# Two-layer graph kernel: first features in halves, first slab as a corner and a rest, eight warming products

## The chip, the cores and the metric

The kernel runs on one core of a Trainium2 chip. The metric is the device time of one execution in microseconds (us); the number shown for a kernel is the median of its runs. A profile is one further execution, recorded by the hardware profiler; the stretch from its first to its last recorded work is the span, and all times in profile lines count from the start of the span.

The core has a matrix engine (PE, "TensorE", whose weight loads are listed apart as PEld), a vector engine (DVE, "VectorE"), a scalar engine (ACT, "ScalarE"), a general engine (POOL) and SP, which here only issues transfers. Transfers between the chip's memory and the core are carried by 16 DMA engines and are issued here from SP's and from ACT's instruction stream (their queues).

## What is computed

Two graph layers on features x of 8 x 2048 x 64 with a normalized adjacency `adj` of 2048 x 2048, each followed by a layer norm over the sum with its input:

```python
def reference(x, adj, L0_gnn_embedding, L0_gnn_weight, L0_gnn_bias, L1_gnn_weight, L1_gnn_bias):
    # layer 0: I, A, 2 A A - I applied to x, node-wise weights from an embedding
    ...
        x_g = jnp.einsum('knm,bmc->bnkc', A_stack, x)
        out = jnp.einsum('bnki,nkio->bno', x_g, w)
        return out + b
    ...
    x = _layernorm(x + _L0_gnn_ref(x, adj, ...), axis=-1)
    # layer 1: x, A x, 2 A A x - x, for two supports (both are adj), shared weights
    x = _layernorm(x + _L1_gnn_ref(x, adj, adj, L1_gnn_weight, L1_gnn_bias), axis=-1)
    return x
```

All entries of a row of `adj` that are not zero are equal, so the kernel multiplies by a matrix of ones and zeros and scales the rows afterwards.

## The kernel before

Features lie in 16 tiles of 128 nodes (partitions) by 512 values (8 batches by 64 channels). `in_x` holds them in this layout; `in_adj` holds the transposed adjacency as [half of the targets, source tile, 128 sources, 1024 targets]. The program has four passes over the adjacency, one after another on PE: the first hop (lines 544 to 613, `hop_x`), the second (seven products of quarters, line 623), the mixing of layer 0 (line 413), and layer 1's two hops (lines 880 and 1011 on).

The change lies wholly in the start of the first hop. `hop_x(g, kk, j)` handles source tile k = kk + 8 j against quarter g of each half of the targets, that is 2 x 512 targets in 8 blocks of 128. In time the sources come in the order 0, 8, 1, 9, 2, 10 and so on, first for g = 0, then for g = 1, together 32 steps. A step has three parts, which `run` (line 279) calls ahead of time by a lead: `features` (lead 4, transfers), `operands` (lead 2, casts) and `use` (lead 0, the products). Instructions of one engine stay in the order in which these parts call them (`ordered`, `keep_in_program_order`).

- **Features.** A float32 tile is split into two parts for the matrix engine: `high` (line 247) copies it on ACT into `hl[0]` in the rounded type fp32r; `low` (line 250) subtracts that on DVE into `hl[1]`. Tile 0 is loaded by `first_constants` (line 134) from ACT's queue, and tile 8 and the later ones from SP's.
- **Slab.** The adjacency rows of the source tile for the 2 x 512 targets are loaded into `raw` and turned into ones and zeros in `s` on DVE. For source tiles 0 and 8 in g = 0 (the branch `if g == 0 and kk == 0`) the two halves of 512 targets are separate transfers (`load_slab` in `features`, line 551) and separate DVE operations (line 562); all later steps load 2 x 512 in one and turn them in one operation (`places`, line 235).
- **Products.** `add_block` (line 262) issues 16 products a step: for each of the 8 blocks i of 128 targets, one with `hl[0]` and one with `hl[1]`, both over 512 columns. In a step they come block by block, high then low; in the first step of a pass (`first`) the eight high ones come before the eight low ones.
- **Warming products.** `first_constants` issues WARM products of a tile of zeros (`idle`) before the first real ones; nobody reads their result, but they occupy the accumulator bank that blocks 6 and 7 use in the first step.
- **Waits of transfers.** `load` (line 124) keeps the order of each queue. The raw slabs share a pool of 6 buffers (RAW), the operands `s` one of 4 and the feature parts `hl` one of 7, so that a later load or cast waits until an earlier buffer has been used.

On SP's queue the order at the start is: the two half slabs of tile 0, the features of tile 8, the two half slabs of tile 8, the features of tile 1, the whole slab of tile 1, the features of tile 9, and so on. On ACT's queue: the features of tile 0 and then the small array `rcol`. ACT then loads its table for the square root (line 139) and runs the casts.

On DVE the order is: half slab 0 of tile 0, low part of tile 0, half slab 1 of tile 0, low part of tile 8, half slabs 0 and 1 of tile 8, slab and low part of tile 1, then the four operations of `put_together` (line 536), which make sums of pairs of slabs for the second hop, and slab and low part of tile 9. On ACT: high parts of tiles 0, 8 and 1, then `seen` (line 601), a counted bf16 copy of each slab, between the later high parts.

Of the kernel before, what the change touches and what calls it, by code (L numbers as in the profile page):

```python
# [14 lines left out]
ALU = mybir.AluOpType  # L15
# [3 lines left out]
P = 128  # L19
B, N, C = 8, 2048, 64  # L20
# [5 lines left out]
FIRST = 8  # L26
HL = 7
RAW = 6
WARM = 10
SLOTS = 3  # L30
SPLIT = 4096.0
SWAPPED = (0, 2, 1, 3, 4, 6, 5, 7)
# [9 lines left out]
def pattern(  # L42
# [22 lines left out]
    nc = tc.nc  # L65
# [20 lines left out]
    def bank(name):  # L86

        return psum.tile([P, 2, 512], F32, tag="ps", name=name)
# [7 lines left out]
    z = [z0, [z1[:, t, :] for t in range(NT)], [z2[:, t, :] for t in range(NT)]]  # L96

    def bc(s, t):
        return z[s][t].rearrange("p (b c) -> p b c", c=C)
# [24 lines left out]
    def load(q, to, src):  # L124
        return tc.keep_in_program_order(q.dma_start(out=to, in_=src))
# [3 lines left out]
    def ordered(ins):  # L129
        if in_order:  # L130
            tc.keep_in_program_order(ins)


    def first_constants():
        load(nc.scalar, z[0][0], x[0].rearrange("n b c -> n (b c)"))
        load(nc.scalar, rcol, rcols)
        nc.vector.memset(eps, EPS)

        tc.keep_in_program_order(nc.scalar.activation(root, eps, AF.Sqrt))

        idle = spool.tile([P, 5 * P], BF16, tag="s", name="idle")
        nc.vector.memset(idle, 0.0)
        first = bank("first")
        for _ in range(WARM):
            nc.tensor.matmul(first[:, 0, :], lhsT=idle[:, :P], rhs=idle[:, P:], start=True, stop=True)
        nc.vector.memset(part, 1.0 / C)
        make_identity(nc, ident)
# [77 lines left out]
    def load_slab(src, shape):  # L225
        raw = rawp.tile(shape, F32, tag="raw", name="raw")
        load(nc.sync, raw, src)
        return raw
# [6 lines left out]
    def places(raw):  # L235
        s = spool.tile(list(raw.shape), F32R, tag="s", name="s")
        ordered(nc.vector.tensor_scalar(s, raw, 0.0, None, ALU.not_equal))
        return s
# [8 lines left out]
    def high(src, to):  # L247
        ordered(nc.scalar.copy(to[0], src))  # L248

    def low(src, to):  # L250

        ordered(nc.vector.tensor_tensor(to[1], src, to[0], ALU.subtract))  # L252

    def halves(src, to=None):

        if to is None:
            to = [hpool.tile([P, B * C], F32R, tag="hl", name="hl") for _ in range(2)]
        high(src, to)
        low(src, to)
        return to  # L260

    def add_block(accs, s, hl, first, last):

        order = [(i, h) for i in range(len(accs)) for h in range(2)]
        if first:
            order.sort(key=lambda ih: ih[1])
        for i, h in order:
            nc.tensor.matmul(  # L268
                accs[i], lhsT=s[:, i * P : (i + 1) * P], rhs=hl[h],
                start=(first and h == 0), stop=(last and h == 1),  # L270
            )
# [19 lines left out]
    def banks(n):  # L291
        pairs = [bank("acc") for _ in range(n // 2)]
        return [p[:, i] for p in pairs for i in range(2)]
# [107 lines left out]
    def centre_features(t):  # L401
        s = work.tile([P, B], F32, tag="ln_s", name="s")
        ordered(nc.vector.tensor_reduce(s, bc(0, t), AX.X, ALU.add))  # L403
        ordered(nc.gpsimd.tensor_tensor(s, s, part, ALU.mult))  # L404
        ordered(nc.gpsimd.tensor_tensor(bc(0, t), bc(0, t), wide(s), ALU.subtract))
# [110 lines left out]
    Q = N // 4  # L516
    BC = B * C // 2
    KK = NT // 2
    first_constants()


# [3 lines left out]
    quarters = scratch.tile([KK, P, 2, 2, Q], BF16, tag="quarters", name="quarters")  # L525
    corner = scratch.tile([KK, P, 2, Q], BF16, tag="corner", name="corner")
    couple, due, stores = [], [], []

    def put_together(g, kk, x0, x1):
        to = z2[:, 2 * (kk % 8) : 2 * (kk % 8) + 2, :].rearrange("p t n -> p (t n)").bitcast(BF16)  # L530
        to = to.rearrange("p (i n) -> p i n", i=4)
        for i, (a, b, op) in enumerate((
            (x0[:, 1], x1[:, 1], ALU.add), (to[:, S1], x0[:, 0], ALU.subtract),
            (x1[:, 0], to[:, S2], ALU.subtract), (x0[:, 0], x0[:, 1], ALU.subtract),
        )):
            ordered(nc.vector.tensor_tensor(to[:, i], a, b, op))

        stores.append(lambda: ordered(nc.scalar.dma_start(out=sums_of[kk, g], in_=to)))

        for _ in range(2):  # L540
            if len(stores) > (1 if g else 6):
                stores.pop(0)()

    def hop_x(g, kk, j):
        k = kk + KK * j

        def features(got):
            if g == 0 and kk == 0:
                if j == 1:
                    load(nc.sync, z[0][k], x[k].rearrange("n b c -> n (b c)"))  # L550
                got["raws"] = [load_slab(adj[h, k, :, :Q], [P, Q]) for h in range(2)]

        def operands(got):
            if g == 0 and kk == 0:

                s = got["s"] = spool.tile([P, 2, Q], F32R, tag="s", name="s")
                hl = got["hl"] = [hpool.tile([P, B * C], F32R, tag="hl", name="hl") for _ in range(2)]
                high(z[0][k], hl)
                if j == 1:
                    low(z[0][k], hl)  # L560
                for h in range(2):
                    ordered(nc.vector.tensor_scalar(s[:, h], got["raws"][h], 0.0, None, ALU.not_equal))
                    if h == 0 and j == 0:
                        low(z[0][k], hl)
            else:
                if g == 0:
                    load(nc.sync, z[0][k], x[k].rearrange("n b c -> n (b c)"))
                raw = load_slab(adj[:, k, :, g * Q : (g + 1) * Q].rearrange("h m n -> m h n"), [P, 2, Q])
                got["s"] = places(raw)
                got["hl"] = halves(z[0][k])  # L570
                if g == 1 and len(loads) > 3:
                    load(nc.sync, *loads.pop(0))
            while due:
                due.pop(0)()
            couple.append(got["s"])
            if j == 1:
                due.append(lambda both=couple[:]: put_together(g, kk, *both))
                couple.clear()
                if g == 1 and kk == KK - 1:
                    due.pop(0)()  # L580

        def out(i):
            t = 4 * g + i if i < 4 else 4 * g + i + 4
            a, r = accs[i], rcol[:, t : t + 1]
            if i % 2 if g == 0 or i > 3 else i > 1:
                ordered(nc.vector.tensor_scalar_mul(z[1][t], a, r))
            else:
                ordered(nc.scalar.activation(z[1][t], a, AF.Copy, scale=r))

        def use(got):  # L590
            s, hl = got["s"], got["hl"]
            if kk == 0 and j == 0:
                accs[:] = banks(8)
            last = kk == KK - 1 and j == 1
            add_block(accs, s.rearrange("p h n -> p (h n)"), hl, kk == 0 and j == 0, last)
            if last:
                for i in range(8 if g == 0 else 4):
                    out(i)
            seen = xcpool.tile([P, 2, Q], BF16, tag="ln_xc", name="seen")
            i = g * NT + k  # L600
            ordered(nc.scalar.activation(seen, s, AF.Copy, accum_out=nonzero[:, i : i + 1]))
            if j == 1:
                ordered(nc.scalar.dma_start(out=quarters[kk, :, :, g, :], in_=seen))
            else:
                ordered(nc.scalar.dma_start(out=corner[kk, :, g, :], in_=seen[:, 0]))
            if k in centred and g == 1:
                centre_features(k)
            if last and g == 1:
                stores.pop(0)()

                todo.extend(lambda i=i: out(i) for i in range(4, 8))

        return [(4, features), (2, operands), (0, use)]


# [142 lines left out]
    accs, centred = [], []  # L758
# [141 lines left out]
    s = ("load_sum", "operands")  # L900
    h, norm = None, None
# [3 lines left out]
    for t in range(NT):  # L905
        got, last = {}, t == NT - 1
# [62 lines left out]
        norm, h = norm_now, z[0][t]  # L969
# [435 lines left out]
def gnn_kernel(tc, x, xT, adj, diag, rcols, bias, pack, w0, out):  # L1405
    nc = tc.nc
    with tc.tile_pool(name="flag", bufs=1) as fpool:
        flag = fpool.tile([1, 1], I32, tag="flag", name="flag")
        odd = pattern(tc, x, xT, adj, diag, rcols, bias, pack, w0, out, flag)
        with tc.If(odd > 0):  # L1410
            general(tc, x, adj, bias, pack, w0, out)
# [45 lines left out]
```

## Time and profile before

| what | value |
|---|---|
| median of 3 runs | 751.47 us (751.16 to 751.69) |
| profiled execution | 751.04 us |
| its span | 749.2 us |
| PE busy | 740.5 us (99% of the span) |
| PEld, DVE, ACT, POOL busy | 613.4, 598.5, 456.6, 293.9 us |
| granted TensorE clock over the span | 0.997 |
| all transfers | 96.47 MB, mean 129 GB/s |
| line 268, products of the first hop (`acc`) | 512, 116.6 us |

How to read it: PE is busy almost all the time, so the order of time along PE is the whole program. Where a line in the profile carries a bracket, it gives the time for which the engine stood idle just before, and what released it. "x47" means that 47 instructions in a row are merged into one line. SPq and ACTq are the instruction streams that issue transfers.

The early transfers and DMA share, in windows of the profile:

```profile
0.00:5.18 5.18, 3.68 (x11) 1.24 (x11) 0.85 (x5) 2.10 (x3) 0.70 (x6) 1.00 0.61 198
5.18:8.00 2.82, 2.82 (x12) 2.13 (x13) 1.95 (x4) 0.62 (x1) 0.00 (x0) 1.00 0.96 300
8.00:12.00 4.00, 4.00 (x19) 3.34 (x18) 1.98 (x5) 2.36 (x5) 0.00 (x0) 1.00 1.01 384
```

The columns are the window, its length, the busy time (and count) of PE, PEld, DVE, ACT and POOL, the granted clock, the mean busy share of the DMA engines, and GB/s.

### The profile page before, as it was taken

What the parts mean: (1) busy time and instruction counts of PE and PEld (TensorE: products, weight loads), DVE (VectorE), ACT (ScalarE), POOL (GpSimd) and SP (SyncE); (2) the same over time, 40 slices, a digit from 0 to 9 for tenths busy, and PEclk for the clock granted to TensorE, in tenths of its full rate; (3) what the DMA queues carried; (4) which work ended last, traced back from release to release, by engine and by line L of the source; (5) the groups of instructions that cost most, each with busy time, mean ns of one, the idle gap of its engine ahead of it and who ended that gap; (6) DMA issues with size and microseconds to landing.
All of it is one profiled execution on the core that took longest, in us unless ns stands there. A gap on an engine that the chain in (4) does not pass through costs nothing.

```text
span 749.2 us, 13523 instructions
## 1 busy us (share of the span) xinstructions
PE 740.5 (99%) x4940; PEld 613.4 (82%) x4940; DVE 598.5 (80%) x952; ACT 456.6 (61%) x1123; POOL 293.9 (39%) x314
## 2 busy tenths in 40 slices
PE   9999999999999999999999999999999999999996
PEld 6888888888888888888888888888888888888885
DVE  6868887999978898888888888869588457778563
ACT  5545453878756678777777777778877662012111
POOL 0001111133233888888888888874000000021431
PEclk9999999999999999999999999999999999999998
DMA  8996997555420000000000000004454454665621
GB/s 301 365 381 214 380 397 243 177 159 166 157 86 15 17 15 16 20 15 26 11 20 15 16 15 1 2 29 131 135 159 151 129 170 139 180 183 171 198 98 46
DMA packets 73544, 96.47 MB, mean 129 GB/s; under 512 B 4864, under 2 KB 48384, under 8 KB 73344
## 3 DMA queue, kind: packets, MB, share of 16 engines
q1 hardware_dynamic: 62064, 76.66, 32.5%
q10 hardware_dynamic: 11408, 18.89, 6.8%
q8 instruction: 41, 0.67, 0.4%
q14 instruction: 31, 0.25, 0.1%
HBM read 76.65 MB, written 18.87 MB: 127 GB/s over the span
## 4 chain that ended last, share of the span: by engine, by line
PE 98%; DMA 0%; DVE 0%; ACT 0%; issue 0%; DVEq 0%; ACTq 0%
PE pm L424 35%; PE accT L705 27%; PE acc L268 16%; PE a L268 10%; PE accT L268 6%; PE pu L499 3%; PE pt L314 1%; PE accT L861 1%; DMA z<-in_x 0%; PE accT L499 0%; PE accT L155 0%; PE accT L314 0%; ACT hl L248 0%; DVE z L303 0%; DVE sq L1076 0%
## 5 line engine op out<-in xcount | busy, mean ns | idle before, releaser
L705 PE MATMUL accT<-s,hl 128*128 128x512 f32 x896 | 205.8, 391 | 0.0
L705 PEld LDWEIGHTS accT<-s,hl 128*128 128x128 f32 x896 | 167.5, 188 | 35.5 <-issue 0.5
L458 ACT ACTIVATE aside<-pm,pack_sb 128x128 f32<-128x128 f32 x512 | 141.9, 437 | 18.9 <-PE pm L424 16.3
L424 PE MATMUL pm<-wh,hl 64*128 64x512 f32 x768 | 151.7, 392 | 0.0
L424 PE MATMUL pm<-wm,parts 64*128 64x512 f32 x768 | 149.8, 387 | 0.0
L424 PE MATMUL pm<-wl,parts 64*128 64x512 f32 x768 | 149.7, 386 | 0.0
L692 ACT CAST s<-raw 128x1024 fp32r<-128x1024 bf16 x104 | 110.1, 1059 | 36.8 <-ACT hl L248 27.9
L268 PE MATMUL acc<-hl,s 128*128 128x512 f32 x512 | 116.6, 390 | 0.2 <-ACT hl L248 0.2
L474 DVE TENSOR_REDUCE sums<-aside 128x128 f32<-128x1024 f32 x96 | 112.6, 1214 | 1.4
L268 PEld LDWEIGHTS acc<-hl,s 128*128 128x128 f32 x512 | 95.8, 188 | 21.0 <-ACT hl L248 0.7
L445 DVE TENSOR_TENSOR aside<-pm,pack_sb 128x1024 f32<-128x1024 f32 x64 | 78.0, 1222 | 18.5 <-PE pm L424 18.1
L424 PEld LDWEIGHTS pm<-wm,parts 64*128 64x128 f32 x768 | 72.0, 184 | 15.3
L424 PEld LDWEIGHTS pm<-wh,hl 64*128 64x128 f32 x768 | 72.2, 185 | 14.7 <-issue 0.4
L424 PEld LDWEIGHTS pm<-wl,parts 64*128 64x128 f32 x768 | 72.2, 184 | 14.4
L248 ACT CAST hl<-z 128x256 fp32r<-128x256 f32 (+1 forms) x96 | 47.9, 517 | 58.6 <-PE acc L268 23.9
L268 PE MATMUL a<-hl,s 128*128 128x512 f32 (+1 forms) x352 | 73.4, 370 | 0.0
L404 POOL TENSOR_TENSOR s<-s,part 128x8 f32<-128x8 f32 x16 | 7.0, 439 | 166.0 <-DVE s L403 95.4
L252 DVE TENSOR_TENSOR hl<-z,hl 128x512 fp32r<-128x512 f32 (+1 forms) x96 | 58.1, 613 | 17.3 <-ACT hl L248 6.9
L463 POOL TENSOR_TENSOR aside<-aside 128x1024 f32<-128x1024 f32 (+2 forms) x48 | 70.9, 1477 | 2.5
L268 PEld LDWEIGHTS a<-hl,s 128*128 128x128 f32 x352 | 61.9, 188 | 11.3
L301 POOL TENSOR_TENSOR z<-z,got 128x512 f32<-128x512 f32 x3 | 4.8, 1631 | 143.4 <-ACT got L300 143.4
L369 ACT ACTIVATE sq<-z 128x512 f32<-128x512 f32 x31 | 20.1, 653 | 48.2 <-DVE z L303 46.9
(139 smaller groups left out, 956.5 us busy)
## 6 DMA issues: line engine op xcount, KB each, us to landing
raw<-in_adj SPq DMA_DIRECT2D x58, 512.0 KB, 6.1
raw<-sums_of SPq DMA_DIRECT2D x64, 256.0 KB, 2.9
sums_of<-z ACTq DMA_DIRECT2D x16, 512.0 KB, 6.9
raw<-quarters SPq DMA_DIRECT2D x32, 256.0 KB, 2.7
raw<-in_adj SPq DMA_DIRECT2D x16, 384.0 KB, 3.5
quarters<-seen ACTq DMA_DIRECT2D x16, 256.0 KB, 6.3
xt<-in_xT SPq DMA_DIRECT2D x16, 256.0 KB, 2.7
z<-in_x SPq DMA_DIRECT2D x15, 256.0 KB, 6.4
```

The lines of the kernel that those rows point to most:

```text
L248: ordered(nc.scalar.copy(to[0], src))
L252: ordered(nc.vector.tensor_tensor(to[1], src, to[0], ALU.subtract))
L268: nc.tensor.matmul(accs[i], lhsT=s[:, i * P : (i + 1) * P], rhs=hl[h], start=(first and h == 0), stop=(last and h == 1),)
L369: ordered(nc.scalar.activation(sq, src, AF.Square))
L424: nc.tensor.matmul(pm[:, j], lhsT=tt[k][n][q, u, :], rhs=w_parts[n][k][q, ds, :], start=(k == 0 and n == 0), stop=(k == 2 and n == 2),)
L445: ordered(nc.vector.tensor_tensor(side_by_side(a), got, e, ALU.mult))
L458: ordered(nc.scalar.activation(to[d], got, AF.Copy, scale=emb_sb[:, t, h * DD + d : h * DD + d + 1]))
L463: ordered(nc.gpsimd.tensor_tensor(to, to, more, ALU.add))
L474: ordered(nc.vector.tensor_reduce(to, src, AX.X, ALU.add))
L499: nc.tensor.matmul(pm[:, j, i * 3 * C : (i + 1) * 3 * C], lhsT=hT[q, 2 * g + i, :], rhs=v[q], start=True, stop=True,)
L692: ordered(nc.scalar.copy(s, got["raw"]))
L705: nc.tensor.matmul(acc[i][:, c], lhsT=hl[h][:, i * P : (i + 1) * P], rhs=S[:, c * 512 : (c + 1) * 512], start=(kk == 0 and h == 0), stop=( ...
```

## The change

Everything concerns tile 0 and tile 8 in g = 0, and the warming products.

1. The features of tile 0 are loaded in two halves of 256 columns, the first from ACT's queue, the second as the first transfer of SP's queue.
2. Tile 0's slab is loaded as a corner (the first 128 targets of both halves, 2 x 128) and a rest (2 x 384) instead of two halves of 512. Tile 8's slab is loaded in one transfer of 2 x 512.
3. The high part of tile 0 is made by two engines: DVE copies columns 256 to 511, ACT columns 0 to 255. The corner is turned in one DVE operation, the rest in two, and the low part of tile 0 follows behind them.
4. For tile 8, the slab is turned in one DVE operation, and its low part, which stood ahead of the slab on DVE, now follows it.
5. In the first step of the first hop the blocks come in the order 0, 4, 1, 2, 3, 5, 6, 7 (blocks 0 and 4 are the corner's).
6. WARM is 8 instead of 10.

The orders that result: on SP's queue, second half of tile 0's features, corner, rest, features of tile 8, slab of tile 8, features of tile 1 and on as before; on DVE, copy of half of tile 0, corner, the two pieces of the rest, low part of tile 0, slab of tile 8, low part of tile 8, slab and low part of tile 1 and on as before. The changed kernel's line numbers are 1 higher at `add_block` and `low`, which is line 253 there.

```diff
-WARM = 10
+WARM = 8
...
     def first_constants():
-        load(nc.scalar, z[0][0], x[0].rearrange("n b c -> n (b c)"))
+        for q, part_of in ((nc.scalar, slice(0, B // 2)), (nc.sync, slice(B // 2, B))):
+            load(q, bc(0, 0)[:, part_of], x[0][:, part_of])
         load(nc.scalar, rcol, rcols)
...
-    def add_block(accs, s, hl, first, last):
+    def add_block(accs, s, hl, first, last, blocks=None):
 
-        order = [(i, h) for i in range(len(accs)) for h in range(2)]
+        order = [(i, h) for i in blocks or range(len(accs)) for h in range(2)]
         if first:
             order.sort(key=lambda ih: ih[1])
...
+    corners = (slice(0, P), slice(P, Q))
...
             if g == 0 and kk == 0:
                 if j == 1:
                     load(nc.sync, z[0][k], x[k].rearrange("n b c -> n (b c)"))
-                got["raws"] = [load_slab(adj[h, k, :, :Q], [P, Q]) for h in range(2)]
+                slab_of = adj[:, k, :, :Q].rearrange("h m n -> m h n")
+                got["raws"] = [load_slab(slab_of[:, :, c], [P, 2, c.stop - c.start]) for c in (corners if j == 0 else (slice(0, Q),))]
...
                 hl = got["hl"] = [hpool.tile([P, B * C], F32R, tag="hl", name="hl") for _ in range(2)]
-                high(z[0][k], hl)
+
+                def place(c, raw):
+                    ordered(nc.vector.tensor_scalar(s[:, :, c], raw, 0.0, None, ALU.not_equal))
+
                 if j == 1:
-                    low(z[0][k], hl)
-                for h in range(2):
-                    ordered(nc.vector.tensor_scalar(s[:, h], got["raws"][h], 0.0, None, ALU.not_equal))
-                    if h == 0 and j == 0:
-                        low(z[0][k], hl)
+                    high(z[0][k], hl)
+                    place(slice(0, Q), got["raws"][0])
+                else:
+                    ordered(nc.vector.tensor_copy(hl[0][:, BC:], z[0][k][:, BC:]))
+                    ordered(nc.scalar.copy(hl[0][:, :BC], z[0][k][:, :BC]))
+                    place(corners[0], got["raws"][0])
+                    for h in range(2):
+                        ordered(nc.vector.tensor_scalar(s[:, h, P:], got["raws"][1][:, h], 0.0, None, ALU.not_equal))
+                low(z[0][k], hl)
             else:
...
             last = kk == KK - 1 and j == 1
-            add_block(accs, s.rearrange("p h n -> p (h n)"), hl, kk == 0 and j == 0, last)
+            first = g == 0 and kk == 0 and j == 0
+            add_block(accs, s.rearrange("p h n -> p (h n)"), hl, kk == 0 and j == 0, last, (0, 4, 1, 2, 3, 5, 6, 7) if first else None)
```

## The prediction

> **What bounds the kernel now.** I read the chain that ended last first, then the page's slices, then the first 13 us of the timeline. The chain (start, length, what) is TensorE nearly throughout:
>
> ```profile
> 0.74 3.75 DMA z<-in_x
> 5.18 116.57 PE acc L268 x512
> 121.75 7.75 PE accT L705 x34
> 130.55 90.44 PE accT L705 x398
> ```
>
> After the first features land, 512 products of line 268 run as one piece of 116.57 us, and the next piece follows at once. Whatever delays or advances the start of this piece moves the end of the kernel by the same amount; inside it only a wait that TensorE itself feels counts. The clock row of the page is 9 (90% or more) in all slices, so nothing is to be had there:
>
> ```profile
> PE   9999999999999999999999999999999999999996
> ...
> PEclk9999999999999999999999999999999999999998
> ```
>
> The start, from the timeline (start, length, engine, line; in brackets the idle time before and what ended it):
>
> ```profile
> 1.28 3.68 PE L145 MATMUL first<-idle 128*128 128x512 bf16 x10 [1.28 <-DVE part L146]
> ...
> 4.32 0.43 DVE L562 TENSOR_SCALAR s<-raw 128x512 fp32r<-128x512 f32 x1 [3.07 <-DMA raw<-in_adj]
> ...
> 4.50 0.62 ACT L248 CAST hl<-z 128x512 fp32r<-128x512 f32 x1 [1.34 <-DMA z<-in_x]
> ...
> 5.16 0.69 DVE L252 TENSOR_TENSOR hl<-z,hl 128x512 fp32r<-128x512 f32 x1 [0.41 <-ACT hl L248]
> 5.17 0.77 PEld L268 LDWEIGHTS acc<-hl,s 128*128 128x128 f32 x4 [0.71 <-ACT hl L248]
> ...
> 5.76 0.42 DVE L562 TENSOR_SCALAR s<-raw 128x512 fp32r<-128x512 f32 x1
> ...
> 6.24 9.84 PEld L268 LDWEIGHTS acc<-hl,s 128*128 128x128 f32 x44 [0.30 <-DVE s L562]
> 6.87 0.69 DVE L252 TENSOR_TENSOR hl<-z,hl 128x512 fp32r<-128x512 f32 x1 [0.68 <-ACT hl L248]
> 7.75 0.43 DVE L562 TENSOR_SCALAR s<-raw 128x512 fp32r<-128x512 f32 x1 [0.19 <-DMA raw<-in_adj]
> ...
> 8.45 0.43 DVE L562 TENSOR_SCALAR s<-raw 128x512 fp32r<-128x512 f32 x1 [0.27 <-DMA raw<-in_adj]
> ...
> 10.62 0.69 DVE L237 TENSOR_SCALAR s<-raw 128x1024 fp32r<-128x1024 f32 x1 [1.75 <-DMA raw<-in_adj]
> ...
> 11.23 0.68 DVE L252 TENSOR_TENSOR hl<-z,hl 128x512 fp32r<-128x512 f32 x1
> ```
>
> Tile 0's features are cast by ScalarE from 4.50, the first product starts at 5.18, four products run, TensorE waits 0.30 us for the second half of the first slab, and from 6.24 it never waits again.
>
> To compare waits at different places I use one measure. From 6.24 to the piece's end at 121.75 there are 508 products: 115.51 / 508 = 0.2274 us each. A product number n (from 0) that cannot start before T would have needed the piece to begin at T - 0.2274 n. The largest such number over all waits, the **equivalent start**, decides the end. Now: product 0 gives 5.18; product 4 gives 6.24 - 0.91 = 5.33; product 16 (tile 8, its first half slab ready at 7.75 + 0.43, plus 0.06 as from 6.18 to 6.24) gives 8.24 - 3.64 = 4.60; product 33 (tile 1's low part, 11.91 + 0.06) gives 11.97 - 7.50 = 4.47; product 49 (tile 9's low part, 15.09 + 0.69 in the timeline) gives 15.84 - 11.14 = 4.70. So 5.33 decides, and the waits behind it have 0.63 us or more in reserve.
>
> **The change part by part.**
>
> *Fewer warming products.* In the trace the ten started 0.43 us apart until 3.82, then at 4.15, 4.37 and 4.58. The two left out are the last two, gone before data is there in either kernel: 0. What covers it is TensorE's wait for tile 0. If that cover went, they would cost two steps of 0.22 us. The Trainium skill, "TensorE: Matmul & The Clock Gate", section "What's actually happening", has a free-running window of 3413 ns that must be busy before the clock rises; here the spacing halved some 2.9 us after the first product, less than a whole window. By the row the change is worth 0; by the rule the clock could rise a window later in an execution with another phase, which I keep as a rival.
>
> *Queues.* SP issues six transfers up to tile 1's features in both kernels, ScalarE two; POOL has nothing to do with the stage. Each issue takes 0.43 us, and SP's third begins at 1.65, while packets flow from about 1.9 us on and are backed up until 8 us (DMA share 0.96 and 1.01 in the windows 5.18 to 8 and 8 to 12). Issue is therefore hidden. Bytes are the same; packets are not. The packet records of the trace have a median of 84 ns for 2048 B, 65 for 1536, 46 for 1024, 27 for 512. For tile 0 and its slab each of 16 engines now has 24 x 84 = 2016 ns; after, 16 x 46 + 16 x 27 + 16 x 65 = 2208 ns. That is +0.19 us for everything queued behind. The skill, "DMA: Bandwidth & Descriptors", section "Issuing engines are not separate DMA queues", says that transfers from several issuing engines interleave on the same 16 DMA engines and save only issue time; by that rule the second queue brings no earlier landing, and the rows below give it none either beyond the smaller size.
>
> *First product.* Its data before: 16 packets of 84 ns (first half slab and features) on each engine, last landing 4.49. After: both feature halves and the corner, 16 x 46 + 16 x 27 = 1168 ns against 1344, so the corner lands at 4.49 - 0.18 = 4.31 and the feature halves, 736 ns, at about 3.9. ScalarE's half cast has a row (line 248, 128x256: 413 ns): ready 4.31. VectorE's copy of the other half has no row; between 0.30 (the 512-wide line 562 at 0.43 and the 1024-wide line 237 at 0.69 give 0.17 + 0.51 ns per element) and 0.54 (line 252, 128x256); it ends by 4.2 to 4.44. The corner's 256 elements take 0.30 by the same line: 4.61, first product 4.66 (up to 4.8). Alone, a gain of 5.33 - 4.66 = 0.67.
>
> *Blocks 0 and 4 first.* Only two products can run; product 2 needs the rest of the slab. Before, its second half landed at 5.54 (last of its 16 semaphore updates); with +0.19, 5.73; I keep 5.54 as the other end. Then 0.02 to start, 384 elements in 0.36, 0.06: 6.17. Equivalent start 6.17 - 0.45 = 5.71 (5.52 with 5.54). Four products stood ahead of this wait before, two do now, and this gives the gain back. Both rest pieces and tile 0's low part follow on VectorE from 5.75 at 0.28, 0.28 and 0.69: product 8 at 7.05, equivalent 5.23, hidden.
>
> *Tile 8, the new wait.* Its slab is now one transfer and one line-562 operation, and VectorE takes the low part after it instead of before (at 6.87). Before, the slab's second half landed at 8.43, needed only by product 24; now all of it is needed by product 16. With +0.19 it lands at 8.62 (other end 8.43): 8.64 + 0.69 + 0.06 = 9.39, equivalent 5.75. Product 17 needs the low part, queued behind: 8.64 + 0.61 (spacing from 10.62 to 11.23) + 0.69 + 0.05 = 9.99, equivalent 9.99 - 3.87 = **6.12** (5.93 with 8.43). Behind it on VectorE stands tile 1's slab, which waits for its own landing until 10.62 anyway.
>
> *Sum.* Equivalent start 5.33 becomes 5.93 to 6.12: +0.60 to +0.79; I take +0.7. Tile 1's and tile 9's waits, 0.19 later, stay below 5. The profiled execution took 751.04 us with a span of 749.2 (1.84 around it), and becomes 751.74; the median of the runs lies 0.43 higher, so I forecast 751.47 + 0.7 = 752.2.
>
> **The rivals.**
>
> *A, the early start pays in full* (faster). The piece starts at 4.66 and stays there: 751.47 - 0.67 = 750.8. It needs the rest of the slab by 4.66 + 0.45 - 0.44 = 4.67 and tile 8's slab by 4.66 + 3.87 - 1.37 = 7.16, where the rows have 5.54 and 8.43. For it: tile 8's slowest two DMA engines land 0.5 to 0.75 us after the others (7.68 against 8.18 and 8.43), a lag that may differ. It shortens the time from a tile-8 landing below 7.83 on (5.33 + 3.87 - 1.37).
>
> *B, it cancels.* Landings come 0.4 to 0.6 us sooner than I take them, about 8.0 and 5.35; equivalent 5.33 to 5.50: 751.5 to 751.6.
>
> *C, the clock rises late.* Eight products end by 4.7 at the slow spacing, then TensorE idles between 5.1 and 6.17. If the clock is low until 10 us, products take 0.427: (9.99 - 6.17) / 0.427 = 9 instead of the 15 due before the tile-8 wait, six late, 6 x 0.2274 = 1.4: 753.6. Against it: in the profile the clock was up by 4.15.
>
> **How the numbers follow.** Forecast 0.66, A 0.08, B 0.18, C 0.06, 0.02 for what I don't see in later stages. The forecast's own range is 751.7 to 752.7 (0.60 to 0.79, with the runs' spread of 0.3 and a landing 0.2 later still); taking in B and half of A gives 751.1 to 753.0. 0.2% is 1.5 us, about what a measurement of this kernel can tell from no change. The gain is capped at 0.67, so faster by more has only the unseen, 0.02; slower by more is C and a tile-8 landing 0.8 later than I take it, 0.09; within, 0.89.
>
> **What would show it.** After: first product near 4.66, a wait before the third until about 6.2 ended by the rest piece, then a wait of some 0.4 us at product 17 ended by line 253's low part of tile 8 near 9.9, and the 512 products ending near 122.4. No wait at products 16 and 17 would make the forecast wrong, and so would a slab of tile 8 that lands before 7.8.

## The result and the profile after

The changed kernel takes 753.70 us (median of 6 runs, 752.90 to 755.35) against 751.32 for the kernel before (6 runs, 750.65 to 752.06): a ratio of 1.0033 with a 95% interval of 1.0023 to 1.0044, 2.4 us more. The forecast was 752.2 in a range of 751.1 to 753.0, so the sign was as forecast and the time lies outside the range. The profiled execution (752.90, span 750.7) is the shortest of the six; that matters below.

The chain that ended last in the changed kernel, in the same columns as before (start, length, what):

```profile
1.65 4.95 DMA raw<-in_adj
7.04 3.89 PE acc L269 x15
10.97 112.56 PE acc L269 x495
123.53 7.79 PE accT L716 x34
```

The 512 products were one piece from 5.18 to 121.75. Now two of them run early and are not on the chain at all, a piece of 15 starts when the rest of tile 0's slab has landed, and 495 start at 10.97. The end of the piece moved by 123.53 - 121.75 = 1.78 us; the span grew by 1.41 (749.25 to 750.66), since the tail after the last product was shorter this time. The start, from the timeline:

```profile
4.58 0.29 DVE L563 TENSOR_SCALAR s<-raw 128x256 fp32r<-128x256 f32 x1 [0.92 <-DMA raw<-in_adj]
...
5.02 0.70 PE L269 MATMUL acc<-hl,s 128*128 128x512 f32 x2
...
6.62 0.63 DVE L573 TENSOR_SCALAR s<-raw 128x384 fp32r<-128x384 f32 x2 [1.75 <-DMA raw<-in_adj]
7.04 3.04 PEld L269 LDWEIGHTS acc<-hl,s 128*128 128x128 f32 x14 [1.75 <-DVE s L573]
...
9.62 0.70 DVE L563 TENSOR_SCALAR s<-raw 128x1024 fp32r<-128x1024 f32 x1 [1.76 <-DMA raw<-in_adj]
10.23 0.69 DVE L253 TENSOR_TENSOR hl<-z,hl 128x512 fp32r<-128x512 f32 x1
...
10.43 0.19 PEld L269 LDWEIGHTS acc<-hl,s 128*128 128x128 f32 x1 [0.35 <-issue]
10.96 5.08 PEld L269 LDWEIGHTS acc<-hl,s 128*128 128x128 f32 x23 [0.35 <-DVE hl L253]
```

The reader should see the forecast's own chain of waits, each where it was said to be: two products from the corner, a wait ended by the rest (line 573), product 16 alone at 10.43, and a short wait at product 17 ended by the low part of tile 8 (line 253). Only the landings are late: the corner is turned at 4.58 instead of 4.31 and the first product starts at 5.02 instead of 4.66, which the later waits hide; the rest is turned at 6.62 instead of 5.75, tile 8's slab at 9.62 instead of 8.64. The equivalent start of product 17 is 10.97 - 3.87 = 7.10, and 7.10 - 5.33 = 1.77 is the whole movement of the piece.

How the transfers ran, in windows (window, length, busy time and count of PE, PEld, DVE, ACT and POOL, clock, mean busy share of the DMA engines, GB/s). Before:

```profile
3.50:4.50 1.00, 1.00 (x5) 0.39 (x4) 0.18 (x1) 0.00 (x0) 0.00 (x0) 1.00 1.04 368
4.50:8.50 4.00, 3.78 (x17) 2.56 (x15) 2.45 (x6) 1.24 (x2) 0.00 (x0) 1.00 0.97 314
```

After:

```profile
3.50:4.50 1.00, 1.00 (x4) 0.20 (x2) 0.16 (x1) 0.40 (x1) 0.00 (x0) 1.00 0.45 121
4.50:8.50 4.00, 2.55 (x9) 1.53 (x9) 1.53 (x4) 0.62 (x1) 0.00 (x0) 1.00 1.04 300
```

From 3.5 to 4.5 the DMA engines are busy 45% of the time and move 121 GB/s instead of 368, although SP had issued the rest by 2.12 and three more transfers behind it. Some 250 KB are lost there, 0.67 us at the rate before. From 4.5 to 8.5 they are busy all the time, 1.04 against 0.97, and still move less, 300 GB/s against 314, because single packets took longer. The median of a 2048 B packet is 84 ns in both kernels, but the mean of those that start in this window is 117 ns after and 99 ns before: 14% of them take over 150 ns, against 8%. So the changed kernel has two losses here, engines that are not given work and packets that take longer.

Only part of the 2.4 us is in this execution. The other part is shown by the second profile of the changed kernel, among the experiments.

### The profile page after: what moved, and what is told of

Read it like the earlier page. It is cut to its first block, busy times and chain, and to the rows that moved or that the text cites. A ratio compares the mean times of both kernels' runs of the same rounds, so it can differ in the third digit from the quotient of the medians.

```text
span 750.7 us, 13518 instructions
## 1 busy us (share of the span) xinstructions
PE 741.0 (99%) x4938; PEld 612.7 (82%) x4938; DVE 598.7 (80%) x953; ACT 457.0 (61%) x1123; POOL 293.7 (39%) x314
## 4 chain that ended last, share of the span: by engine, by line
PE 98%; DMA 1%; DVE 0%; SPq 0%; issue 0%; ACT 0%; DVEq 0%; ACTq 0%
PE pm L425 35%; PE accT L716 27%; PE acc L269 16%; PE a L269 10%; PE accT L269 6%; PE pu L500 3%; PE pt L315 1%; DMA raw<-in_adj 1%; PE accT L872 1%; PE accT L500 0%; PE accT L156 0%; SPq L125 0%; PE accT L315 0%; DVE z L304 0%; DVE sq L1087 0%
## 5 line engine op out<-in xcount | busy, mean ns | idle before, releaser
L249 ACT CAST hl<-z 128x512 fp32r<-128x512 f32 (+1 forms) x95 | 47.2, 516 | 60.1 <-PE acc L269 26.4
```

## The experiments

Five theories went in, by the letters used in the expectations. L: the main loss is the low part of tile 8, moved behind its slab. D: the many small packets of corner and rest delay every slab. F: the second feature half at the head of SP's queue does. W or C: eight warming products and the idle time behind them make the clock rise late or fall back. Later, T: tile 8's slab in one transfer lands later; I: it takes two parts together. Ratios are against the kernel before, measured alongside on the same chip.

### One part undone

**u1_halves**: tile 0's slab in halves of 512, blocks in natural order, the low part of tile 0 between the halves as in the kernel before.

```diff
-got["raws"] = [load_slab(slab_of[:, :, c], [P, 2, c.stop - c.start]) for c in (corners if j == 0 else (slice(0, Q),))]
+if j == 0:
+    got["raws"] = [load_slab(adj[h, k, :, :Q], [P, Q]) for h in range(2)]
+else:
+    got["raws"] = [load_slab(slab_of, [P, 2, Q])]
...
```

> Tile 0's slab in two halves of 512 as before (128 packets of 2048 B each), all else as changed. Three theories. D (the rest piece and all transfers behind it land about 1 us late because corner and rest are 256 small packets each): the second half lands near 5.5 and tile 8's slab near 8.5, equivalent start 5.9 to 6.1, span 0.9 to 1.2 us shorter than the changed kernel's 750.7, median about 752.0. L (the low part of tile 8 moved behind its slab is the main loss): tile 8 still waits, median within 0.3 of the changed kernel's 753.7. W (eight warming products let the clock rise late): no change, 753.7.

Measured: 752.82 (11 runs), ratio 1.0020 (1.0011 to 1.0029). Tile 0's second half is turned at 5.94, tile 8's slab only at 9.84. Corner and rest are not what holds tile 8's slab back, against D. Nor is the stretch of idle DMA engines from 3.5 to 4.5, which is not there:

```profile
3.50:4.50 1.00, 1.00 (x4) 0.20 (x2) 0.33 (x2) 0.41 (x1) 0.00 (x0) 1.00 1.06 280
4.50:8.50 4.00, 3.62 (x14) 2.40 (x14) 1.41 (x3) 0.62 (x1) 0.00 (x0) 1.00 0.95 258
```

The packets are long all the same: those of 2048 B that start from 4.5 to 8.5 have a mean of 119 ns. Product 17 decides again, at 11.18, equivalent 7.31. The median lies between the 752.0 of D and the 753.7 of L and W. What made it shorter than the changed kernel's is not shown; TensorE's idle time before the second half is 0.24 us here, where the changed kernel has 1.32 before the rest.

**u2_tile8**: tile 8 in two transfers and two operations, its low part ahead of them.

```diff
-got["raws"] = [load_slab(slab_of[:, :, c], [P, 2, c.stop - c.start]) for c in (corners if j == 0 else (slice(0, Q),))]
+if j == 0:
+    got["raws"] = [load_slab(slab_of[:, :, c], [P, 2, c.stop - c.start]) for c in corners]
+else:
+    got["raws"] = [load_slab(adj[h, k, :, :Q], [P, Q]) for h in range(2)]
...
 if j == 1:
     high(z[0][k], hl)
-    place(slice(0, Q), got["raws"][0])
+    low(z[0][k], hl)
+    for h in range(2):
+        ordered(nc.vector.tensor_scalar(s[:, h], got["raws"][h], 0.0, None, ALU.not_equal))
```

> Tile 8's slab in two transfers and two operations again, its low part ahead of them, all else as changed. D: the third product still waits until about 7.0 for the rest (equivalent start 6.6), nothing waits at tile 8, so 0.5 us less than the changed kernel: median about 753.2. L: equivalent start back to about 5.5, median about 752.0. W: 753.7.

Measured: 755.18 (5 runs: 752.62, then 755.02 to 755.99), ratio 1.0057 (1.0044 to 1.0071). The profiled execution is the one of 752.62 and goes as D said: no wait at tile 8, product 2 at 6.90 (equivalent 6.45). The other four are 2.4 to 3.4 us longer, with a mean granted clock of 0.995 against 0.997. In the two profiles the equivalent start goes from 7.10 to 6.45, so the order of tile 8 is worth about what L gave it, 0.6 us, and is not the main loss. The change that removed a wait made the kernel slower; what these four runs did was not profiled.

**u3_warm10**: `WARM = 10`.

> Ten warming products again, all else as changed. D and L: the first real product starts up to 0.3 us later, but products 2 and 17 wait as long as in the changed kernel: median 753.7, within 0.4. W: the loss that is not in the changed kernel's profiled execution (its median lies 0.8 above it) goes away, median 752.9 or less, and the spread of the runs shrinks to that of the kernel before (1.4 us).

Measured: 753.11 (11 runs, 752.00 to 754.81), ratio 1.0026 (1.0017 to 1.0035). Product 2 waits until 7.13, product 17 until 11.08, as in the changed kernel. The two longest runs (754.44, 754.81) have a granted clock of 0.995, the rest 0.997 or 0.998. The median lies between what the theories gave.

**u4_features**: tile 0's features in one transfer on ACT's queue, cast by ACT.

```diff
-for q, part_of in ((nc.scalar, slice(0, B // 2)), (nc.sync, slice(B // 2, B))):
-    load(q, bc(0, 0)[:, part_of], x[0][:, part_of])
+load(nc.scalar, z[0][0], x[0].rearrange("n b c -> n (b c)"))
...
-ordered(nc.vector.tensor_copy(hl[0][:, BC:], z[0][k][:, BC:]))
-ordered(nc.scalar.copy(hl[0][:, :BC], z[0][k][:, :BC]))
+high(z[0][k], hl)
```

> Tile 0's features in one transfer on ACT's queue and cast by ACT alone, corner and rest as changed. D: SP's queue starts with the corner, so the rest comes one issue (0.45 us) sooner, product 2 near 6.6, tile 8 about 0.3 us sooner: median about 753.2. L: unchanged, 753.7. If the two queues with feature halves were the loss, the median would fall to about 752.

Measured: 751.86 (11 runs), ratio 1.0010 (1.0001 to 1.0019): undoing this one part takes back most of the loss. The rest is turned at 6.06 and tile 8's slab at 8.07. Its windows of transfers, to be held against the two above:

```profile
3.50:4.50 1.00, 1.00 (x4) 0.20 (x2) 0.00 (x0) 0.00 (x0) 0.00 (x0) 1.00 0.94 310
4.50:8.50 4.00, 3.38 (x8) 2.14 (x8) 1.95 (x5) 1.23 (x2) 0.00 (x0) 1.00 1.05 379
```

The hole from 3.5 to 4.5 is gone, and at the same busy share as in the changed kernel, 1.05 against 1.04, the later rate is 379 GB/s instead of 300: 2048 B packets have a mean of 90 ns there instead of 117. The 16 DMA engines bring their parts of tile 8's slab between 7.48 and 8.05; in the changed kernel they do so between 7.82 and 9.60, twelve of them by 8.57. The twelfth is 0.7 us later than in u4_features and the last 1.55, so four late engines make over half of the delay. The eleven runs fall into eight of 751.19 to 751.95 and three of 752.99 to 753.45, and the profile is of one of the three. Its products, in windows of 3.41 us:

```profile
5.92:9.33 3.41, 3.41 (x9) 2.36 (x9) 2.49 (x5) 1.20 (x3) 0.00 (x0) 1.00 1.03 383
9.33:12.74 3.41, 3.41 (x17) 2.78 (x16) 2.62 (x5) 2.76 (x6) 0.00 (x0) 1.00 1.05 390
```

PE never idles in either window, but nine products pass in the first and seventeen in the second: the products ran at the slow spacing until 9.33. The clock column prints 1.00 for both because the record of the clock has its first entry only at that rise; before it, the count has to be read.

### One part alone

**o1_features** and **o3_tile8**: the kernel before with the feature halves alone, and with tile 8's one transfer and order alone (the diffs of u4 and u2 the other way round).

> The kernel before with one part of the change: tile 0's features in halves on two queues, cast by two engines. Theory F (the second feature half at the head of SP's queue makes every slab behind it land 1 to 1.5 us later): tile 8's second half slab lands at 9.2 or later instead of 8.43, product 4 or product 24 waits, median 0.5 to 1.2 above the kernel before. Theory D (only the many small packets of corner and rest delay the slabs): landings as before, product 0 earlier, median equal to the kernel before or 0.2 below.

> The kernel before with one part of the change: tile 8's slab in one transfer and one operation, its low part behind it. Theory L: slab at 8.43, product 17 not before 9.8, equivalent start 5.93 instead of 5.33, median 0.6 above the kernel before. F and D: landings as before, and the same 0.6 from the order alone, or less where the slab lands before 7.9.

Measured: o1_features 752.00 (11 runs), ratio 1.0004 (0.9995 to 1.0013); tile 8's second half turned at 8.10, no wait from the slabs. o3_tile8 752.10 (11 runs), ratio 1.0010 (1.0001 to 1.0019). Its profile shows the two waits that the prediction gave for tile 8, product 16 at 9.93 and product 17 at 10.43:

```profile
9.09 0.69 DVE L563 TENSOR_SCALAR s<-raw 128x1024 fp32r<-128x1024 f32 x1 [2.75 <-DMA raw<-in_adj]
9.69 0.69 DVE L252 TENSOR_TENSOR hl<-z,hl 128x512 fp32r<-128x512 f32 x1
...
9.93 2.41 PE L268 MATMUL acc<-hl,s 128*128 128x512 f32 x8 [0.50 <-DVE s L563]
10.43 1.70 PEld L268 LDWEIGHTS acc<-hl,s 128*128 128x128 f32 x8 [0.35 <-DVE hl L252]
```

The median's 0.57 over the kernel before lies at the 0.6 that L and the forecast's lower end gave for this order, but with the slab at 8.43. In this profile it landed at 9.06, and product 17's equivalent start is 10.43 - 3.87 = 6.56, 1.23 over 5.33; a second execution (o3b, below) had the slab at 8.26, product 17 at 9.63 and took 751.29 against 751.31. So the order has a price that moves with the landing, and 0.57 is not a measurement of 0.60. F for the half alone falls with o1's first profile.

### The clock

**w14_after** (`WARM = 14`) and **after2**, the changed kernel once more.

> The changed kernel with 14 warming products, which keep TensorE busy until 5.7 to 7.3, about as long as product 2 has to wait anyway. Theory C (TensorE's idle time between 4.7 and 7 makes the clock rise late or fall back in some executions): the runs that stand 1 to 2.5 us above the shortest go away, median 752.9 or less, spread under 1.6 us. If the landings alone decide, the median stays at 753.4 to 754.

> The changed kernel once more, for a second profile of it. Landing theories F and D: rest piece at 6.3 to 6.9, tile 8's slab at 9.2 or later, a second time. If the late landings of the first profile were an accident of that execution, the rest lands near 5.7 and the slab near 8.6, and only the clock can make the median.

Measured: w14_after 753.04 (8 runs, 752.63 to 754.01), ratio 1.0022 (1.0012 to 1.0033); after2 754.18 (5 runs, 753.23 to 754.44), ratio 1.0034 (1.0021 to 1.0047). Measured alongside each other, six more warming products make the kernel 1.14 us shorter, though the wait that decides is the changed kernel's (tile 8 turned at 9.62, product 17 at 10.97; the rest, at 5.91, decides nothing here). The two intervals overlap, but four of the five runs of after2 are longer than all eight of w14_after. C was met in part: the median is 0.14 over its 752.9, and 753.75 and 754.01 still stand over 1 us above the shortest. In the profiles the 512 products end at 123.59 in w14_after, at 123.53 in the first profile of the changed kernel and at 124.94 in after2, where tile 8's slab was turned 0.17 later than in the first. The profile of after2 (754.43) shows what they prevent. TensorE's pieces, then windows:

```profile
4.38 1.04 PE L269 MATMUL acc<-hl,s 128*128 128x512 f32 x2
7.36 8.93 PE L269 MATMUL acc<-hl,s 128*128 128x512 f32 x31 [1.94 <-DVE s L573]
```

```profile
4.93:8.34 3.41, 1.47 (x6) 0.92 (x6) 1.23 (x3) 0.47 (x1) 0.00 (x0) 1.00 1.04 272
8.34:11.76 3.42, 3.42 (x9) 2.64 (x9) 1.29 (x2) 1.44 (x3) 0.00 (x0) 0.50 1.04 398
11.76:15.17 3.41, 3.41 (x16) 2.81 (x15) 3.27 (x6) 2.30 (x6) 0.00 (x0) 1.00 1.05 387
```

TensorE idles 1.94 us for the rest of the slab, is busy 1.47 of 3.41 us, and the granted clock is 0.50 for the next 3.42: nine products instead of the sixteen of the window after. In the first profile of the changed kernel the same wait was shorter, 1.32 us, and the clock did not fall (2.02 of 3.41 us busy from 4.95 to 8.36).

The first rise of the clock moves by itself from one execution to the next. The trace's record of it begins at 4.05, 4.76 and 4.34 us in before, before2 and best1 and at 5.74, 6.50 and 7.23 in o3b, o1_features and o1b, all with ten warming products; until then products start 0.43 us apart.

**u4_warm10**: u4 with `WARM = 10`.

> Features in one transfer on ACT's queue and cast by ACT, corner, rest and tile 8 as changed, ten warming products. Theory C: ten slow products end at 5.55, where the first real product starts, so TensorE has no idle window before the clock rises; the three of eleven runs near 753.2 that the same kernel with eight has (its profile has the clock low until 9.33) go away, median 751.7 to 752.0, spread under 1.5 us. If the clock was not the reason, two or three of the runs stand at 753 again.

Measured: 751.55 (11 runs, 751.38 to 752.13), ratio 1.0005 (0.9996 to 1.0013). The three runs near 753 are gone, as C said: two warming products more, and nothing else, against u4. None of eleven here against three of eleven there, on another chip, is little by the count alone; that the long runs were the clock rests on the profile of u4. With the feature half and the warming products both taken back, the kernel stands 0.2 us above the kernel before, which its interval does not tell from none.

### The queue

**m_rows128**: corner and rest each in two transfers of 128 rows.

```diff
...
+raw = rawp.tile([P, 2, c.stop - c.start], F32, tag="raw", name="raw")
...
+for h in range(2) if j == 0 else ():
+    load(nc.sync, raw[:, h], slab_of[:, h, c])
```

> The changed kernel with corner and rest each in two transfers of 128 rows (one for each half of the targets), the same packets in the same order, two more issues on SP's queue. If the DMA engines stand idle from 3.5 to 4.4 because a transfer of 256 short rows is handed to them late, the hole closes, the rest lands near 5.8, product 2 near 6.2, median about 752.9. If the number of packets or the feature half ahead of them is what counts, the rest stays at 6.5 or later (two more issues of 0.45 us), median 753.7 to 754.3.

Measured: 753.57 (5 runs), ratio 1.0034 (1.0022 to 1.0047). The DMA share from 3.5 to 4.5 is 0.71 (0.69 in after2, with the transfers of the changed kernel), and tile 8's slab is turned at 10.76, so rows for each transfer are not what holds that slab back. For the rest it is open: its two pieces are turned at 5.40 and 6.12, sooner than 6.62, but w14_after has the rest at 5.91 with unchanged transfers.

**m_act2**: both feature halves on ACT's queue.

```diff
-((nc.scalar, slice(0, B // 2)), (nc.sync, slice(B // 2, B)))
+((nc.scalar, slice(0, B // 2)), (nc.scalar, slice(B // 2, B)))
```

> The changed kernel with both feature halves on ACT's queue, so that SP's queue begins with the corner; both halves are still cast by two engines. If the feature half at the head of SP's queue is what delays the slabs, they land as in the kernel with the features in one transfer: rest near 6.0, tile 8's slab near 8.1, median about 752. If halves of 1024-byte rows are, whatever the queue: rest at 6.5 and slab at 9.5, median 753.7.

Measured: 753.30 (7 runs, 751.58 to 754.99), ratio 1.0028 (1.0017 to 1.0040). The landing of tile 8's slab is that of u4: turned at 8.04, with 324 GB/s from 3.5 to 4.5 and 379 from 4.5 to 8.5. So it is the place on SP's queue, ahead of the slabs, not the halves. That place also makes SP issue the slabs later, but o1_features has this too (tile 8's issued by 3.51 instead of 3.03 before) and its slab is not late. But ACT's queue brings the second half late:

```profile
5.80 0.29 DVE L569 CAST hl<-z 128x256 fp32r<-128x256 f32 x1 [4.56 <-DMA z<-in_x]
...
6.44 6.84 PE L269 MATMUL acc<-hl,s 128*128 128x512 f32 x29 [1.56 <-DVE s L563]
```

TensorE idles 1.56 us before the first product, and five of the seven runs are over 753. The expected median of 752 was a miss; the landing was not.

**before2, o1b, o3b, u1_warm10**: one profile each, to tell single landings from chance. u1_warm10 is u1 with ten warming products.

> The kernel before once more, for a second landing of its slabs. Tile 0's second half slab within 0.25 us of 5.54 and tile 8's second half between 7.9 and 8.6 if landings repeat; a spread of 1 us would make the single landings of all profiles worthless as evidence.

> Feature halves on two queues alone, a second profile. Theory F (the half at the head of SP's queue alone delays the slabs): tile 8's second half at 9.2 or later this time, the first profile's 8.1 having been chance. Theory I (it takes the half at SP's head and tile 8 in one transfer, or the corner, together): 8.0 to 8.6 again.

> Tile 8's slab in one transfer alone, a second profile. Theory T (one transfer of 512 KB lands later than two of 256 KB): 8.9 to 9.2 again, as in the first (9.07). If that was chance: 8.1 to 8.6.

> Feature halves on two queues and tile 8's slab in one transfer, tile 0's slab in halves, ten warming products: the two parts together, without the corner. Theory I: slab at 9.5 or later, as in the first profile of this pair (9.82). If each part adds its own delay by itself: about 8.7 to 9.1.

Measured, with all other profiles: the start of the operation that turns the last of tile 8's slab, in us.

| half at SP's head | corner and rest | tile 8 in one transfer | kernels | turned at |
|---|---|---|---|---|
| no | no | no | before, before2, best1 | 8.45, 7.87, 8.10 |
| no | no | yes | o3_tile8, o3b | 9.09, 8.28 |
| no | yes | yes | u4_features, u4_warm10, m_act2 | 8.07, 8.37, 8.04 |
| yes | no | no | o1_features, o1b | 8.10, 8.64 |
| yes | no | yes | u1_halves, u1_warm10 | 9.84, 9.03 |
| yes | yes | no | u2_tile8 | 9.48 |
| yes | yes | yes | after, after2, u3_warm10, w14_after | 9.62, 9.79, 9.73, 9.62 |
| yes | in 128 rows | yes | m_rows128 | 10.76 |

These starts repeat within 0.8 us. In before2 and best1 VectorE was the later one; before2's slab had landed at 7.54, sooner than expected and 0.9 sooner than in before. T is chance (9.09, then 8.28). The half alone stays below 8.7 twice; with either other part it is 9.03 or more in all eight profiles; without the half, no kernel is above 9.1 and the mean of the eight is 8.28. That the half on SP's queue makes the slab late in the changed kernel is shown by undoing it: 8.04 to 8.37 in three profiles, against 9.62 to 9.79 in four. That it needs a second part for this, theory I, is likely and not shown: u1_warm10's 9.03 misses I's 9.5 and lies where delays that simply add were expected, and 8.64 and 9.03 are nearer to each other than two profiles of one kernel can be. Why the engines then idle, and why their packets take longer, is not shown and stays open.

### A version to beat both

**best1**: the kernel before with tile 0's low part behind its second half slab.

```diff
-if h == 0 and j == 0:
-    low(z[0][k], hl)
+if j == 0:
+    low(z[0][k], hl)
```

> The kernel before with one change: tile 0's low part follows its second half slab on VectorE instead of standing between the halves. Product 4 then waits for 5.56 + 0.43 + 0.06 = 6.05 instead of 6.24; equivalent start 5.18 instead of 5.33: 0.15 us less than the kernel before, which the runs cannot tell from no change, and no wait before product 4 or one under 0.2 us in the profile.

Measured: 750.99 (11 runs, 750.50 to 751.41) against 751.35 (24 runs), ratio 0.9996 (0.9987 to 1.0005): no difference that these runs can tell. The profile doesn't show the gain either; the second half landed at 5.76 this time, just when VectorE would have been free in the old order:

```profile
5.76 0.43 DVE L562 TENSOR_SCALAR s<-raw 128x512 fp32r<-128x512 f32 x1 [1.01 <-DMA raw<-in_adj]
...
6.24 5.77 PEld L268 LDWEIGHTS acc<-hl,s 128*128 128x128 f32 x26 [0.29 <-DVE s L562]
```

No version tried is shown to be faster than the kernel before.

## Why the prediction was wrong

*What bounds the kernel* held: the piece ended 1.78 us later, its equivalent start moved by 1.77, and no later stage gave anything back or took more, but for the shorter tail. One reading there was wrong: the clock row prints full speed where the trace has no record yet. Before's record begins at 4.05, and until then products start 0.43 us apart.

*The order of waits* held to the last: product 2, 16, 17, with the releasers that were named; product 0 came 0.36 later than forecast and decided nothing. o3_tile8 agrees with the price of the moved low part and the single operation, 0.57 in the median where 0.60 was the lower end, partly by luck, since landings there differ by 0.8.

*The queue term failed.* "+0.19 us for everything queued behind" took the DMA engines as always busy and each packet at its median. Both failed. The engines were busy 0.45 of the time from 3.5 to 4.5, and from 4.5 to 8.5 the mean 2048 B packet took 117 ns, where the count has 84 and the kernel before had 99; for the 24 such packets that each engine brings of tile 8's features and slab that is 24 x 18 ns = 0.43 us more than before, an estimate. Measured, the rest landed 1.06 later than the second half slab before (6.60 against 5.54) and tile 8's slab 1.17 later (9.60 against 8.43). With the measured landings the forecast's own sum gives 9.62 + 0.61 + 0.69 + 0.05 - 3.87 = 7.10, which is what the chain shows. The sentence "Issue is therefore hidden" missed that, here, a transfer at the head of SP's queue makes the ones behind it late though they are issued in time. The Trainium skill's rule cited there, from "DMA: Bandwidth & Descriptors", section "Issuing engines are not separate DMA queues", speaks of saving issue time alone; u4_features and m_act2 differ from the changed kernel in the queue or form of one 128 KB transfer and have tile 8's slab 1.5 us sooner, so here the choice of queue did more than that, and the measurement decides.

*Rival C had the right kind of loss and too little chance.* It had 0.06, against "in the profile the clock was up by 4.15". That was one profile of the kernel before, whose ten warming products leave 0.22 us before the first real one; the rise moves between executions, the change itself makes the idle time that endangers the clock, and the late landing made it longer. I put only a late rise into C; after2 shows a fall back after a rise, and u4_features a late rise. Against w14_after, measured alongside, this is 754.18 - 753.04 = 1.14 us of the median, where C took 1.4. That C's 753.6 lies next to the measured 753.70 is luck: C had the landings of the forecast, about 1 us too early, and a late clock in every execution. The Trainium skill, "TensorE: Matmul & The Clock Gate", section "What's actually happening", has the clock return to half after an idle window of about 3.4 us; after2 lost it with 1.94 us idle at a stretch and 43% of the window busy (1.47 of 3.41), so one whole idle window is not needed.

*The sum*: 1.51 (w14_after over the kernel before, put down to landings and order) and 1.14 (after2 over w14_after, put down to the clock) make the 2.65 by which the changed kernel stood above the kernel before there. The split is an estimate, since w14_after's longest runs may have lost clock too. The 0 for the two products left out was right for products that run into a wait; for the clock it was not safe: u4 with ten instead of eight had none of the long runs that were three of eleven.

## What to carry to other kernels

An early start that is followed by a wait is worth nothing if the wait's end decides; put the first wait's data first, and count how many products stand ahead of it. Idle time of TensorE near the start has two prices, the time itself and the clock, so warming work should reach the first stretch that is not interrupted again, not only the first product. A term for transfers needs a row in which the engines were handed that sequence; median packet times alone are its lower end, since a few slow packets on a few engines decide when the whole transfer has landed.

## What was not expected

- With every transfer issued well ahead, the DMA engines of the changed kernel were busy 0.45 of the time from 3.5 to 4.5 us (0.69 in after2), against 0.94 in u4_features and 1.04 in the kernel before. In u1_halves it is 1.06, and tile 8's slab is as late.
- The median 2048 B packet takes 84 ns in every profile. The mean from 4.5 to 8.5 us is 117 to 128 ns in the four profiles of the changed kernel with 8, 10 or 14 warming products, and 88 to 90 where the feature half is off SP's queue (u4_features, u4_warm10, m_act2).
- A wait of 1.94 us took the granted clock to 0.50 for 3.42 us; one of 1.32 us did not.
- Removing the tile-8 wait (u2_tile8) left four of five runs at 755 or more. That longer idle time costs the clock there too is argued from the granted clock of 0.995, not shown; 0.002 of 750 us is 1.5 us, less than the 2.4 to 3.4 us by which these runs are longer, so something more is in them.
